# The first batch's counting products dealt between the raw groups' products of a graph layer

## The chip, the cores and the metric

The kernel runs on one core of a Trainium2 chip. The metric is the device time of one execution in microseconds; of several runs the median is taken. TensorE is called PE in the profile, its weight loads PEld, VectorE DVE, ScalarE ACT, GpSimd POOL, and the queue of SyncE that issues plain transfers SP.

## The reference

There are 12500 nodes with 128 features and 200000 edges, sorted by their target. Every row of x is normalized and clipped at zero; every edge takes the row of its source through the matrix of its type (four types, 128 x 128) and adds the result, with the type's bias, to its target; x itself is added.

```python
h = jnp.maximum(_layernorm(x, axis=-1), 0.0)
xs = h[src]
for i in range(4):
    mask = (edge_type == i)[:, None]
    msgs = msgs + jnp.where(mask, xs @ W[i] + b[i], 0.0)
out = x + jax.ops.segment_sum(msgs, dst, num_segments=N)
```

The targets are drawn with a square, so the first few hundred nodes receive many edges each and the last ones few.

## The kernel before, in words

Edges are cut into chunks of 128. The first 512 chunks, whose targets have many edges, are handled as **dense** work; the other 1051 chunks go by **groups** of 16 (at the end smaller ones).

**The table.** At the start every row of x is normalized and split into three bf16 parts, and written to a table in device memory, htab (`first_part` to `third_part`, L481 to L508). While it is made, `make_slots` (L797) sorts the dense edges into slots of at most 128 edges of one target; loT and hkT hold, for each slot, where the sources of its edges lie.

**Raw groups.** The first three groups (RAW = 3) don't wait for the table. Their rows come straight from x (`gather_raw`, L525, tile hx), and `add_up_raw` (L610) does the rest for each group in steps that are separated by `yield`: statistics on DVE (L440 to L449), a one-hot matrix ohf on DVE (L620); then the scales (L455, L456) and 16 normalizing instructions on ACT (L461); then four times four f32 products of 16 edge chunks on PE (L635), each four copied from PSUM to SBUF by ACT (L636); then the counts of edges per type (L641, copied by L643), and last the bias and the four type matrices (L646, L648), which add into one PSUM bank, raw_py. Two PSUM banks (pool s_ps) take the results of L635 and L641 in turn. A copy on ACT (L1283) brings raw_py to SBUF, and DVE adds it to a ring of target columns later (L666).

**Dense work.** It goes in 18 batches, the first of 17 units and the others of 27. `count` (L938) makes for each slot two one-hots on DVE (o2 at L957, o1 at L961 or L965) and one **counting product** on PE (L983, 128 x 396 columns); a unit is two to four slots in one PSUM bank, copied to the batch's counts tile by ACT (L989). The one-hots go through four sets of buffers of four slots (SETS, SLOTS): a set is made ahead, and one is made again when PE has used it. The first batch has 34 slots. `multiply` (L1021) then streams the whole table from device memory in tiles hs (L1029, four buffers) and multiplies it with the counts (L1033). `dense_work` (L1094) deals the counting of a batch and the multiplying of the batch before it into one stream; each step of it returns the share of the dense work that is done. A slot of the first batch, which has no multiplying beside it, counts 3.5 times in that share.

**The loop.** From group 3 on, each group gathers the rows of its chunks from htab on POOL (`gather`, L538, L544; 12 buffers of two chunks), makes 16 one-hots on DVE (L561), multiplies on PE (`sum_up`, L569, L578), and is weighed one group later (`weigh`, L586: L596, L600, L603, L605); DVE adds the results to the ring (L666). After each two chunks the loop draws steps of the dense work until the share done has come up to `pace` (L1079), which spreads the dense work evenly over the loop. The loop's instructions on PE, DVE and ACT run in the order in which they are written (`manual_schedule`, L1302); what stands ahead of it, the raw groups among it, is ordered by the scheduler.

**Memory.** SBUF is given out by pools that stand on two stacks, a left and a right one. What is needed only at the start lies on the left (early: prep, nodes, aheads, raws) and is freed at L1269; the pools of the loop (outp, later, dense with two counts tiles, sdp, op1, op2, hsp) then take its place on the left. So a tile of theirs must wait for the last reader of the early tile that lay there; the raw rows (pool raws, L247) were the topmost. Two of the waits are of interest: the load of the loop's first block of edge data (`prep_steps`, L306, into pool later; read on DVE by L319 to L329) and DVE's third ohf, of which there are two buffers (L619).

Of the kernel before, what the change touches and what calls it, by code (L numbers as in the profile page):

```python
# [35 lines left out]
F32 = mybir.dt.float32  # L36
# [3 lines left out]
I32 = mybir.dt.int32  # L40
# [8 lines left out]
P = 128  # L49
EPS = 1e-5  # L50
UN = 3
G = 16
# [4 lines left out]
UB = 27  # L57
# [4 lines left out]
STREAM = 4  # L62
# [3 lines left out]
HG = 2  # L66
RAW = 3
LEAD = RAW
SOON = (RAW * 16) + HG

TURN = 4


@with_exitstack
def kernel(
# [170 lines left out]
    aheads = early.enter_context(tc.tile_pool(name="aheads", bufs=4))  # L246
    rawp = early.enter_context(tc.tile_pool(name="raws", bufs=RAW * G // HG))  # L247

# [137 lines left out]
    nc.vector.tensor_single_scalar(iota_1, iota_b, 1.0, op=ALU.add)  # L386
    iota_f = prep.tile([P, KR], F32, name="iota_f", bufs=1)
    nc.vector.tensor_copy(iota_f, iota_i[:, :KR])
# [28 lines left out]

    pick_f = prep.tile([P, NT, N3], F32, name="pick_f", bufs=1)
    nc.vector.tensor_copy(pick_f, pick)
# [190 lines left out]
    def add_up_raw(t0, g, rows, marked):  # L610
# [7 lines left out]
        root()  # L618
        oh = rawp.tile([P, G, KR], F32, name="ohf", bufs=2)[:, :, :K]  # L619
        nc.vector.tensor_tensor(  # L620
# [473 lines left out]
    def dense_work():  # L1094
# [8 lines left out]
        for vs in batches + [None]:  # L1103
            steps, led = {}, {}
            now = None
            if vs:
                now = vs, dense.tile([P, NW + 1, UB * NT], I32, name="counts")
                steps[count(*now)] = sum(len(slots_of(u)) for u in vs) * (a_slot if before else alone_slot)
            if before:
                passed = multiply(*before)  # L1110
                steps[passed] = 3 * len(before[0]) * a_node
                led = {passed: BEHIND}
            done = {st: 0.0 for st in steps}
            while done:
                st = min(done, key=lambda st: done[st] + led.get(st, 0.0))
                part = next(st, None)
                if part is None:
                    del done[st]
                    gone += steps[st]
                else:  # L1120
                    done[st] = part
                    yield (gone + sum(done[st] * steps[st] for st in done)) / total
            before = now
# [9 lines left out]
    hkT = slots.tile([P, NS], F32, name="hkT")  # L1133
    byT = slots.tile([P, (ND - PAIRS) // 2], F32, name="byT")
    building = ExitStack()
    dix = building.enter_context(tc.tile_pool(name="dix", bufs=1, side="right"))
# [129 lines left out]
    for g in groups:  # L1266
        for _ in g:
            pass
    early.close()  # L1269
# [4 lines left out]
    counting = mid.enter_context(ExitStack())  # L1274
    dense = counting.enter_context(tc.tile_pool(name="dense", bufs=2))
    sdp = counting.enter_context(tc.tile_pool(name="sdp", bufs=1))
# [3 lines left out]
    nc.vector.memset(o2s[:, :, :, NB:], 1.0)  # L1280
    hsp = counting.enter_context(tc.tile_pool(name="hsp", bufs=STREAM))
    raw_sums = outp.tile([P, OT, D], F32, name="xo").rearrange("p j d -> p (j d)")[:, : RAW * G * win_raw]
    nc.scalar.copy(raw_sums, raw_py[:, : RAW * G * win_raw])  # L1283
    raw_adds = [
# [17 lines left out]
    ordered.enter_context(tc.manual_schedule(engines={mybir.EngineType.PE, DVE, mybir.EngineType.Activation}))  # L1302
    assert min(goes) >= RAW
    for gi, (t0, g) in list(enumerate(zip(starts, sizes)))[RAW:]:
        q = (t0 + 8 * G) // P
# [15 lines left out]
        for j, part in enumerate(sum_up(t0, g, *now, gi >= FULL)):  # L1321
            late, tails[:] = list(tails), []
            while work and spent < pace(gi, part):
                spent = next(work, None)
                if spent is None:
                    work = None
# [194 lines left out]
```

## Time and profile before

| | us |
|---|---|
| median of the runs shown (1666.21, 1667.36, 1667.64) | 1667.36 |
| the profiled execution | 1663.02 |
| its span in the profile | 1661.2 |
| PE busy in it | 1417.4 (85%) |
| DVE busy | 1014.6 (61%) |
| ACT busy | 446.9 (27%) |
| POOL busy | 1030.6 (62%) |
| mean granted clock of PE | 0.958 |

The span is the time from the first to the last instruction that the profile shows. A line of a timeline has start, duration, engine, line of the kernel, operation, tiles, shape and count, and in brackets how long the engine sat idle before it and what ended that. The f32 products stand as two records each. Records of PE are pipelined: the distance from one start to the next is what one costs, not its duration. A line of busy time by stretch has the stretch, its length, the busy time and count of PE, PEld, DVE, ACT and POOL, the granted clock as a share of the full one, the share of the DMA engines and GB/s.

### The profile page before, as it was taken

To read this page: it belongs to the slowest core of one execution; us is meant where nothing else is said; L and a number is where in the kernel's file an instruction comes from. 1 tells how busy PE (TensorE), PEld (TensorE's weight loads), DVE (VectorE), ACT (ScalarE), POOL (GpSimd) and SP (SyncE) were. 2 spreads that over 40 slices of the span, in tenths; PEclk is the share of its full clock that TensorE was granted. 3 is DMA by queue.
4 is the path that set the end of the run, shared out by engine and by line. 5 is a ranking of instruction groups with operands and counts; after the bars stand their busy time and mean duration, and the time that the engine had idled before them with its cause. 6 is when DMAs were issued, how large, how long until landed. Compare 5 with 4: busy or idle time off the path is not lost.

```text
span 1661.2 us, 32454 instructions
## 1 busy us (share of the span) xinstructions
PE 1417.4 (85%) x10984; PEld 921.7 (55%) x10984; DVE 1014.6 (61%) x5305; ACT 446.9 (27%) x1095; POOL 1030.6 (62%) x1078
## 2 busy tenths in 40 slices
PE   3868798988888889898979899998898889898975
PEld 1336565655555556565555556565565555555644
DVE  6982877647474746574756565666466556563433
ACT  5694222221212122222222222222222222222111
POOL 6435666666666666666666666666666666666562
PEclk9986899999999999999999999999999999999997
DMA  6552476665665656656656565665565556556652
GB/s 204 168 197 75 153 229 194 205 212 185 196 205 182 200 176 211 204 184 199 202 168 199 185 194 187 198 194 188 190 205 185 193 185 193 185 181 192 206 165 63
DMA packets 136761, 308.90 MB, mean 186 GB/s; under 512 B 25899, under 2 KB 78813, under 8 KB 136590
## 3 DMA queue, kind: packets, MB, share of 16 engines
q1 hardware_dynamic: 86909, 204.98, 37.8%
q0 software_dynamic: 49680, 101.81, 20.4%
q8 instruction: 86, 1.41, 0.3%
q14 instruction: 86, 0.70, 0.1%
HBM read 290.65 MB, written 16.04 MB: 185 GB/s over the span
## 4 chain that ended last, share of the span: by engine, by line
PE 74%; DVE 11%; issue 9%; another core or an unknown queue 2%; ACT 1%; DMA 1%; POOL 0%; SPq 0%; DVEq 0%; ACTq 0%; POOLq 0%
PE pa L1033 43%; PE pt L983 11%; PE ps L578 6%; PE py L605 6%; DVE o L957 2%; DVE o L965 2%; PE pt L1047 1%; DVE ring L666 1%; DVE oh L561 1%; PE ps L635 1%; PE py L596 1%; PE pt L691 1%; DVE stt L440 1%; POOL hm L544 0%
## 5 line engine op out<-in xcount | busy, mean ns | idle before, releaser
L544 POOL DMA_INDIRECT hm<-htab,srcT x1003 | 975.0, 972 | 565.5 <-issue 230.9
L1033 PE MATMUL pa<-counts,hs 128*128 128x324 fp8e4 (+1 forms) x5292 | 963.3, 305 | 79.2 <-issue 69.7
L1033 PEld LDWEIGHTS <-hs 128*128 128x128 bf16 x5292 | 492.3, 97 | 353.9 <-issue 132.7
L957 DVE TENSOR_SCALAR o<-iota_n,hkT 128x392 bf16<-128x392 f16 x1167 | 385.0, 330 | 75.2 <-PE pt L983 30.2
L983 PE MATMUL pt<-o,o 128*128 128x396 bf16 x1167 | 369.5, 337 | 40.3 <-DVE o L965 21.4
L989 ACT CAST counts<-pt 128x396 int32<-128x396 f32 x476 | 228.5, 493 | 479.4 <-PE pt L983 149.0
L561 DVE TENSOR_SCALAR oh<-iota_b,keyT 128x56 bf16<-128x56 bf16 (+8 forms) x1003 | 172.8, 260 | 294.6 <-PE ps L578 101.3
L581 ACT COPY sb<-ps 128x224 f32<-128x224 f32 (+8 forms) x251 | 99.4, 397 | 544.5 <-PE pt L983 172.5
L578 PE MATMUL ps<-oh,hm 128*128 128x56 bf16 (+8 forms) x3009 | 192.1, 197 | 38.9 <-issue 32.7
L666 DVE TENSOR_TENSOR ring<-ring,py 128x14 f32 (+7 forms) x976 | 171.9, 176 | 84.4 <-remote 17.3
L578 PEld LDWEIGHTS <-hm 128*128 128x128 bf16 x3009 | 165.2, 99 | 100.4 <-issue 55.1
L965 DVE TENSOR_SCALAR o<-iota,loT 128x128 bf16<-128x128 bf16 x644 | 177.2, 275 | 0.0
L983 PEld LDWEIGHTS <-o 128*128 128x128 bf16 x1167 | 111.3, 98 | 98.9 <-issue 30.2
L965 DVE TENSOR_SCALAR o<-iota,loT,byT 128x128 bf16<-128x128 bf16 x417 | 142.0, 340 | 0.0
L605 PE MATMUL py<-sb,wsb 128*128 128x224 f32 (+7 forms) x488 | 128.3, 402 | 5.5 <-issue 5.3
L605 PEld LDWEIGHTS py<-sb,wsb 128*128 128x128 f32 x488 | 86.4, 190 | 32.9 <-issue 11.7
L528 POOL DMA_INDIRECT hx<-in_x_dram,srcT x48 | 50.1, 1044 | 36.8 <-DVE stt L440 13.1
L997 DVE COPY bi<-counts 128x27 int32<-128x27 int32 (+1 forms) x18 | 4.1, 225 | 107.2 <-ACT counts L989 60.5
L600 ACT CAST cnt<-py 128x224 bf16<-128x224 f32 (+7 forms) x61 | 24.1, 395 | 103.7 <-PE ps L578 35.6
L461 ACT ACTIVATE h<-hm,nmrt,rstdt 128x128 f32<-128x128 f32 x98 | 42.8, 492 | 0.9 <-issue 0.5
L490 PE MATMUL ps<-h,ident 128*128 128x384 f32 (+1 forms) x34 | 17.2, 591 | 15.7 <-issue 11.4
L596 PE MATMUL py<-oh,three 128*32 128x224 bf16 (+7 forms) x244 | 21.2, 311 | 7.6 <-issue 3.9
(234 smaller groups left out, 650.2 us busy)
## 6 DMA issues: line engine op xcount, KB each, us to landing
hs<-htab SPq DMA_DIRECT2D x288, 576.0 KB
hm<-htab,srcT POOLq DMA_INDIRECT x1003
htab<-h SPq DMA_DIRECT2D x32, 288.0 KB
xo<-in_x_dram SPq DMA_DIRECT2D x23, 256.0 KB
out_dram<-xo SPq DMA_DIRECT2D x23, 256.0 KB
hm<-in_x_dram SPq DMA_DIRECT2D x18, 192.0 KB
hs<-htab SPq DMA_DIRECT2D x18, 192.0 KB
hm<-in_x_dram SPq DMA_DIRECT2D x14, 168.0 KB
```

What stands on the lines that cost most here:

```text
L528: one = nc.gpsimd.indirect_dma_start(out=hm[:, i * D : (i + 1) * D], out_offset=None, in_=x, in_offset=bass.IndirectOffsetOnAxis(ap=srcf[: ...
L544: one = nc.gpsimd.indirect_dma_start(out=hm[:, (i - h0) * D3 : (i - h0 + 1) * D3], out_offset=None, in_=htab, in_offset=bass.IndirectOffse ...
L561: nc.vector.tensor_scalar(oh[:, i, :], iota_b[:, :K], keyf[:, at : at + 1], None, ALU.is_equal)
L578: nc.tensor.matmul(ps[:, i - i0, :], rows(i, c), oh[:, i, :], start=(c == 0), stop=(c == 2))
L581: nc.scalar.copy(sb[:, i0:i1].rearrange("p g t n -> p g (t n)"), ps[:, : i1 - i0, :])
L605: nc.tensor.matmul(py[:, :g, :], wsb[:, t, :], sb[:, :g, t, :], start=False, stop=(t == NT - 1))
L666: nc.vector.tensor_tensor(to, to, of(i), ALU.add)
L957: one = nc.vector.tensor_scalar(o2[:, k, :NB], iota_n, hkT[:, s : s + 1], None, ALU.is_equal)
L965: one = nc.vector.tensor_scalar(o1[:, k], iota_1, loT[:, s : s + 1], by, ALU.is_equal, ALU.mult)
L983: one = nc.tensor.matmul(pb, o1, o2, start=first, stop=last)
L989: nc.scalar.copy(counts[:, :, i * NT : (i + 1) * NT], pb.rearrange("p (b t) -> p b t", t=NT))
L1033: nc.tensor.matmul(pa[:, : 3 * nu * NT].rearrange("p (m v) -> p m v", m=3), hs[:, j - j0, c * D : (c + 1) * D], of, start=(j == 0 and c == 0),
```

## The change

The pool of the raw rows moves to the right stack, below the pool of the slots' making, and gets a third ohf buffer; iota_f and pick_f, which the raw groups read, become constants. Ahead of the loop each raw group is taken through two steps only (statistics and one-hot; scales and normalizing). Its other six steps are taken after the order written by hand has begun, and after each of them two steps of the dense work are drawn (AMONG = 2), 32 of the first batch's 34 in all: two counting products after each four raw products, after L641 and after L648. The raw rows are then freed, and only then the second counts tile (dense2) and the hs buffers are given out. `pace` is stretched over the share that is left.

```diff
+AMONG = 2
...
-    rawp = early.enter_context(tc.tile_pool(name="raws", bufs=RAW * G // HG))
...
-    iota_f = prep.tile([P, KR], F32, name="iota_f", bufs=1)
+    iota_f = const.tile([P, KR], F32, name="iota_f")
...
-    pick_f = prep.tile([P, NT, N3], F32, name="pick_f", bufs=1)
+    pick_f = const.tile([P, NT, N3], F32, name="pick_f")
...
-        oh = rawp.tile([P, G, KR], F32, name="ohf", bufs=2)[:, :, :K]
+        oh = rawp.tile([P, G, KR], F32, name="ohf", bufs=RAW)[:, :, :K]
...
-                now = vs, dense.tile([P, NW + 1, UB * NT], I32, name="counts")
+                now = vs, dense[batches.index(vs) % 2].tile([P, NW + 1, UB * NT], I32, name="counts")
...
+    raw_stack = ExitStack()
+    rawp = raw_stack.enter_context(tc.tile_pool(name="raws", bufs=RAW * G // HG, side="right"))
...
     for g in groups:
-        for _ in g:
-            pass
+        next(g)
+        next(g)
...
-    dense = counting.enter_context(tc.tile_pool(name="dense", bufs=2))
...
-    hsp = counting.enter_context(tc.tile_pool(name="hsp", bufs=STREAM))
+    dense = [counting.enter_context(tc.tile_pool(name="dense", bufs=1))]
...
-    nc.scalar.copy(raw_sums, raw_py[:, : RAW * G * win_raw])
...
+    first_slots = sum(len(slots_of(u)) for u in batches[0]) - 2
+    for g in groups:
+        for _ in g:
+            for _ in range(max(0, min(AMONG, first_slots))):
+                spent = next(work)
+            first_slots -= AMONG
+    nc.scalar.copy(raw_sums, raw_py[:, : RAW * G * win_raw])
+    raw_stack.close()
+    dense.append(counting.enter_context(tc.tile_pool(name="dense2", bufs=1)))
+    hsp = counting.enter_context(tc.tile_pool(name="hsp", bufs=STREAM))
+    ahead_of = spent
...
-            while work and spent < pace(gi, part):
+            while work and spent < ahead_of + (1.0 - ahead_of) * pace(gi, part):
```

## Prediction

> **What bounds the kernel now.** I read the page first, then busy time by stretch, then the timelines of PE, DVE and ACT from 110 to 200 us, where the diff acts.
>
> ```profile
> span 1661.2 us, 32454 instructions
> PE 1417.4 (85%) x10984; PEld 921.7 (55%) x10984; DVE 1014.6 (61%) x5305; ACT 446.9 (27%) x1095; POOL 1030.6 (62%) x1078
> ```
>
> PE is the bound over the whole run (85%). The change adds and removes no product, so it can win only PE idle time and PE time at the half clock. Where these lie near the edit:
>
> ```profile
> 120.00:150.00 30.00, 29.14 (x122) 24.90 (x122) 0.83 (x1) 16.61 (x48) 18.36 (x20) 0.50 0.25 72
> 150.00:155.40 5.40, 4.02 (x20) 2.76 (x19) 0.23 (x1) 0.77 (x2) 2.42 (x3) 0.50 0.39 103
> 155.40:180.60 25.20, 13.13 (x110) 6.44 (x108) 19.28 (x97) 9.32 (x24) 16.53 (x17) 0.84 0.29 80
> 180.60:200.00 19.40, 17.81 (x171) 14.44 (x171) 18.73 (x103) 4.58 (x13) 13.01 (x14) 0.92 0.60 191
> ```
>
> The columns are PE, PEld, DVE, ACT and POOL busy, then the granted clock. From 120 to 150 the raw groups run: PE is busy 29.14 of 30 us, but at clock 0.50, and DVE does nothing (0.83). From 155.4 to 180.6 it is the reverse: DVE is busy 19.28 of 25.2, and PE sits idle 12.1 us. Why DVE was idle and then late:
>
> ```profile
> 127.60 0.83 DVE L620 TENSOR_TENSOR ohf<-iota_f,keyT 128x640 f32<-128x640 f32 x1 [7.87 <-PE ps L641]
> 154.16 0.23 DVE L319 CAST sf<-si 128x128 f32<-128x128 int32 x1 [25.74 <-DMA si<-in_src_dram]
> 156.50 0.15 DVE L320 CAST head<-di 128x1 f32<-128x1 int32 x1 [2.11 <-DMA di<-in_dst_dram]
> 158.14 0.32 DVE L957 TENSOR_SCALAR o<-iota_n,hkT 128x392 bf16<-128x392 f16 x1
> 158.59 0.32 DVE L957 TENSOR_SCALAR o<-iota_n,hkT 128x392 bf16<-128x392 f16 x1
> ```
>
> L620 waits for a third ohf buffer; then L319 waits 25.74 us for a load into memory that lay under the raw rows. Behind it in DVE's queue stand the one-hots of the counting products, one slot per 0.45 us (158.14 to 158.59). So the first batch's 34 slots come at DVE's pace, after the raw stage.
>
> **The change, part by part.** P is four raw products, S is two counting products, pc is L641, py is L646 with L648. The rows that price them:
>
> ```profile
> 114.91 3.63 PE L635 MATMUL ps<-ohf,hx 128*128 128x40 f32 x16 [2.44 <-ACT hx L461]
> 120.86 3.64 PE L635 MATMUL ps<-ohf,hx 128*128 128x40 f32 x16 [2.31 <-ACT hx L461]
> 124.42 2.31 PE L641 MATMUL ps<-ohf,pick_f 128*12 128x160 f32 x8
> 126.66 1.93 PE L635 MATMUL ps<-ohf,hx 128*128 128x40 f32 x8
> 128.53 0.31 PE L646 MATMUL pa<-cnt,b 12*128 12x160 bf16 x1
> 128.76 2.50 PE L648 MATMUL pa<-sb,wsb 128*128 128x160 f32 x8
> 131.06 5.31 PE L635 MATMUL ps<-ohf,hx 128*128 128x40 f32 x24
> 148.04 2.31 PE L641 MATMUL ps<-ohf,pick_f 128*12 128x160 f32 x8
> 152.71 0.29 PE L646 MATMUL pa<-cnt,b 12*128 12x160 bf16 x1 [1.38 <-ACT cnt L643]
> 157.07 0.67 PE L983 MATMUL pt<-o,o 128*128 128x396 bf16 x3
> 157.57 0.31 PE L578 MATMUL ps<-oh,hm 128*128 128x40 bf16 x6
> ```
>
> At clock 0.50, from start to start: P 1.78 us (half of 120.86 to 124.42; two records a product), pc 2.24, py 2.53 (128.53 to 131.06). At full clock a counting product takes 0.167 us (157.07 to 157.57, three of them), so S is 0.33 us, and 0.66 at half. In full, P is 0.89, pc 1.12, py 1.27.
>
> *ACT's new order (a loss).* Each group is now run through its normalizing (two steps) before any product, so on ACT all 48 L461 stand ahead of the first copy of a result (L636). Before, only 16 did:
>
> ```profile
> 114.37 6.27 ACT L461 ACTIVATE hx<-hx,nmrr,rstdr 128x128 f32<-128x128 f32 x16 [0.18 <-DVE nmrr L456]
> 120.54 0.45 ACT L636 COPY sb<-ps 128x160 f32<-128x160 f32 x2
> 127.59 0.28 ACT L643 CAST cnt<-ps 12x160 bf16<-12x160 f32 x1 [1.79 <-PE ps L641]
> 152.38 0.28 ACT L643 CAST cnt<-ps 12x160 bf16<-12x160 f32 x1 [3.94 <-PE pt L983]
> ```
>
> One L461 takes 0.385 us ((6.27 - 0.49)/15), 48 of them from 114.37 last to 133.0, and with one copy the third P starts at 133.3 instead of 120.86. The result banks are two, so PE does two P and two S by 120 and then waits 13 us. Nothing hides this.
>
> *Raw stage on PE.* Group 0 has left two P with S, pc, S, py, S. Between pc and py the copy L643 comes; it started 0.93 us after pc's end in one group (126.66 to 127.59) and 2.1 in another (148.04 + 2.24 = 150.28 to 152.38), S hides 0.66, so a gap of 0 to 1.8; I take 0.6, and 1.0 where no S stands. At half clock: 2 x 2.44 + 2.24 + 0.66 + 0.6 + 2.53 + 0.66 = 11.6, to 144.9. The rest hangs on the clock, next. Full: group 1 takes 4 x 1.22 + 1.12 + 0.33 + 0.6 + 1.27 + 0.33 = 8.5, group 2 (its last two steps carry no S) 4.9 + 1.1 + 1.0 + 1.3 = 8.3, and the stage ends at 161.7. Half: 16.5 and 15.5, end 176.9. Before, it ended at 155.2 (2.5 after 152.71).
>
> *The clock.*
>
> ```profile
> 139.33:142.74 3.41, 3.41 (x15) 3.19 (x15) 0.00 (x0) 3.41 (x10) 2.54 (x3) 0.50 0.18 49
> 152.98:156.40 3.42, 3.42 (x18) 2.78 (x18) 0.23 (x1) 1.31 (x3) 1.55 (x2) 0.50 0.68 186
> 159.81:163.22 3.41, 1.76 (x20) 0.99 (x20) 3.41 (x19) 0.69 (x2) 2.50 (x4) 1.00 0.26 70
> 163.22:166.64 3.42, 1.23 (x12) 0.54 (x11) 3.42 (x19) 0.59 (x2) 2.81 (x3) 1.00 0.31 85
> 1641.20:1644.61 3.41, 3.41 (x18) 2.67 (x16) 1.15 (x2) 0.51 (x1) 0.00 (x0) 0.50 0.27 77
> ```
>
> The granted clock changes only at steps of 3.413 us. For every such window I counted the columns put through (f32 twice) against what the window's clock could carry. The 20 half-clock windows that ended at half had a share of 0 to 0.74 (139.33 is the 0.74); the 20 after which it rose had 0.78 to 1.15 (152.98 has 0.90, the last, 1641.20, has 1.04). At full clock, 159.81 (0.45) kept it and 163.22 (0.22) lost it; the losing ones lie at 0.46 and below, 19 of 21 at 0.36 and below, and after the first 20 us of the run none that kept it lies under 0.38. PE's busy time doesn't tell these apart, the columns do. P alone has a share of 0.30 (8 records x 80 columns in 1.78 us, at 396/0.33 = 1.2 columns a ns), so the raw stage never rose. With S it is (640 + 792)/2928 = 0.49: too little to rise, enough to keep. But S, pc, S in a row is 3.56 us at 0.97, and py, S nearly as long: wherever the window falls, one of them mostly fills it. So I take a rise in group 0's pc or py, about 145, kept from there: three chances in four.
>
> The Trainium skill (TensorE: Matmul & The Clock Gate, "What's actually happening") says instead that about 3.4 us of sustained activity of the PE releases the throttle. By that rule the 29.14 busy us above would not have stayed at 0.50; the trace disagrees, and the rule's own result is a rival below.
>
> *After the raw stage.* What before has done at 180.6 beyond the raw groups is some 46 counting products and 66 L578 (42 and 60 from 155.4 on, and a few ahead). The changed kernel still has 14 and 66 of them.
>
> ```profile
> L578 PE MATMUL ps<-oh,hm 128*128 128x40 bf16 x60 | 3.4, 191 | 0.0
> L561 DVE TENSOR_SCALAR oh<-iota_b,keyT 128x56 bf16<-128x56 bf16 (+8 forms) x1003 | 172.8, 260 | 294.6 <-PE ps L578 101.3
> 169.65 1.40 DVE L666 TENSOR_TENSOR ring<-ring,xo 128x10 f32 x7
> ```
>
> PE: 14 x 0.167 + 66 x 0.057 = 6.1. DVE has its one-hots 12 or so slots ahead (four sets of buffers), and still owes L319 to L329 (1.9), 16 L561 (2.8 at 0.17) and 7 adds (1.4), 6.1 as well. I take 6.5. That is 161.7 + 6.5 = 168.2 against 180.6: **12.4 us earlier**. It counts as won the PE stall that ends there:
>
> ```profile
> 175.90 0.85 PE L983 MATMUL pt<-o,o 128*128 128x396 bf16 x4 [1.28 <-DVE o L965]
> 180.59 0.67 PE L1033 MATMUL pa<-counts,hs 128*128 128x204 fp8e4 x3 [3.84 <-issue]
> 178.34 0.29 ACT L600 CAST cnt<-py 128x160 bf16<-128x160 f32 x1 [3.79 <-remote]
> 180.05 0.89 ACT L989 CAST counts<-pt 128x396 int32<-128x396 f32 x2
> ```
>
> L1033 needs the last L989 of the first batch, which stood in ACT's queue behind L600 (178.34); the first of the two ends at 180.54, and L1033 starts at 180.59. In the new order that L989 is ahead of any L600.
>
> *The queues.* The four hs loads now wait until the raw rows are free:
>
> ```profile
> 112.63 1.75 SPq L1029 DMA_DIRECT2D hs<-htab x4
> L544 POOL DMA_INDIRECT hm<-htab,srcT x24: 940/946/1080, 114.7 to 149.6; - x24
> ```
>
> Before, SP issued them at 112.63. Now it is at the last pc, some 2.5 us before the stage's end, and the first L1033 comes some 3 us after it. A cost of 0 to 4 us; I take 2. SP has nothing urgent behind them. POOL's 24 gathers into 12 buffers were done by 150.5 and are as early now; the later ones wait for L578, as before. The side load (si, ty, di) moves ahead of two table writes on SP and is long landed. Bringing iota_f and pick_f to the constants, and the split of the counts into two pools, issue nothing new.
>
> Sum: -12.4 + 2 = **-10**. The other 1480 us keep their order and work (the dense share per group falls as the first batch is gone, by as much as was moved). The profiled execution took 1663.0 us (span 1661.2), so 1653; the median shown is 1667.4, some 4 above it, and I apply the 10 to that: **1657.4**.
>
> **Rivals.**
> 1. *The clock never rises in the raw stage (slower).* Price: end at 176.9, + 6.5 + 1.7 for a window at half + 2 = 187.1 against 180.6, **+6.5: 1674**. For: P with S has 0.49, and gaps before py near 1.8 empty the windows; against: S, pc, S leaves only some phases under 0.75. It decides where the stage ends after 172.
> 2. *The rise comes only in group 1.* End near 169.5, so -2 to -3: **1665**, the idle 13 us ahead having eaten the gain.
> 3. *The 3.84 us stall comes again*, since its root, a late L600, may be of PE's and not of this order: -6, **1661**.
> 4. *PE rises on busy time alone*, in the first window after 133.3, by 138.2: group 0's pc on at full, end at 158.6, 3.1 earlier: -13, **1654**. The row of 120 to 150 speaks against it. It is what the rule of the Trainium skill (TensorE: Matmul & The Clock Gate, "What's actually happening") would give.
>
> **How the numbers follow.** Forecast 0.42, rival 1 0.20, rival 2 0.15, rival 3 0.18, rival 4 0.05. A measurement can tell about 0.2% (3.3 us). Faster: 0.42 + 0.18 + 0.05 = 0.65; same: rival 2, 0.15; slower: rival 1, 0.20. The forecast's own range is 1653 to 1661 (L643's gap 0 to 1.8 in three groups, the loads 0 to 4). To leave out no more than 2 in 10 the range goes to 1652 below, and above into rival 1, to 1671.
>
> **What would show it.** ACT: 48 L461 without a copy among them, ending near 133. PE: a gap of about 13 us from 120, L983 between L635 from then on, last L648 near 162 (or 177). The clock: 1.00 by 145 to 148; if it is 0.50 up to 170, rival 1 holds. DVE: no wait of 25 us at L319. First L1033 some 3 us after the last L648, with no stall of 3.8 us; if it waits for hs, the loads were late. If the stage ends near 162 and the gain is still missing, DVE is the bound after it, and my 6.5 us were wrong.

## The result, and the profile after

The changed kernel is slower: 1692.7 us median (1687.4 to 1694.2) against 1667.5 (1666.2 to 1668.6), 1.0146 times, 95% interval 1.0128 to 1.0163. Its profiled execution took 1687.4 us, 24.4 more than that of the kernel before. The prediction said 10 us less, and its range ended at 1671.

The page of the changed kernel shows no more work, only more time in which PE waits:

```profile
span 1685.7 us, 32466 instructions
PE 1420.3 (84%) x10984; PEld 922.9 (55%) x10984; DVE 1019.6 (60%) x5305; ACT 448.2 (27%) x1095; POOL 1033.0 (61%) x1078
```

ACT's timeline in the raw stage (start, duration, engine, line, tiles, count, and in brackets the idle time ahead with its cause) has the 48 L461 in one row, as forecast, and then something that was not forecast:

```profile
115.47 18.57 ACT L461 ACTIVATE hx<-hx,nmrr,rstdr 128x128 f32<-128x128 f32 x48 [0.33 <-DVE nmrr L456]
...
149.02 0.29 ACT L636 COPY sb<-ps 128x160 f32<-128x160 f32 x1 [11.64 <-remote]
150.43 0.49 ACT L989 CAST counts<-pt 128x396 int32<-128x396 f32 x1 [1.11 <-remote]
150.81 0.28 ACT L643 CAST cnt<-ps 12x160 bf16<-12x160 f32 x1
```

PE's timeline beside it:

```profile
134.27 1.93 PE L635 MATMUL ps<-ohf,hx 128*128 128x40 f32 x8 [13.38 <-ACT sb L636]
136.00 0.86 PE L983 MATMUL pt<-o,o 128*128 128x396 bf16 x2
136.65 1.77 PE L635 MATMUL ps<-ohf,hx 128*128 128x40 f32 x8
...
151.14 0.29 PE L646 MATMUL pa<-cnt,b 12*128 12x160 bf16 x1 [9.05 <-ACT cnt L643]
...
174.68 1.35 PE L648 MATMUL pa<-sb,wsb 128*128 128x160 f32 x8
175.87 0.31 PE L578 MATMUL ps<-oh,hm 128*128 128x40 bf16 x6
...
178.34 0.43 PE L1033 MATMUL pa<-counts,hs 128*128 128x204 fp8e4 x3
```

There are two gaps. The first, 13.38 us, is ACT's row. The second, 9.05 us, is odd: by its records PE was through with the fourth four raw products (from 136.65) by 138.4, and ACT copied them only at 149.02 ("remote": the profile finds no instruction that ended this wait). The clock came late as well. Busy time by stretch (columns as in the prediction):

```profile
134.00:151.00 17.00, 7.82 (x30) 5.12 (x31) 0.57 (x3) 2.82 (x11) 9.84 (x11) 0.50 0.25 67
151.00:166.00 15.00, 14.86 (x61) 11.60 (x60) 5.74 (x26) 4.37 (x12) 0.00 (x0) 0.50 0.01 2
166.00:176.00 10.00, 9.57 (x76) 7.74 (x75) 4.22 (x20) 4.38 (x11) 0.00 (x0) 0.97 0.09 12
```

So the raw stage ended at 176.0, not at 161.7. Yet the dense work, on which the prediction was built, is not late: the first L1033 comes at 178.34, and in the kernel before it came at 180.59. What is late is the loop. Its first copy of a group's counts stood at 178.34 in the kernel before; here it is

```profile
203.04 0.29 ACT L600 CAST cnt<-py 128x160 bf16<-128x160 f32 x1 [1.25 <-PE ps L578]
```

24.7 us later, and the last L600, 64 groups on, is 24.5 us later (1650.9 and 1675.4). All that was lost was lost by the first group. The engine that shows where is the one that the prediction passed by, POOL, which gathers the loop's rows. POOL's timeline, first before, then after:

```profile
149.58 0.95 POOL L544 DMA_INDIRECT hm<-htab,srcT  x1 [0.30 <-issue]
152.63 0.95 POOL L544 DMA_INDIRECT hm<-htab,srcT  x1 [2.10 <-PE pt L983]
```

```profile
145.93 0.95 POOL L544 DMA_INDIRECT hm<-htab,srcT  x1 [0.30 <-issue]
176.45 0.95 POOL L544 DMA_INDIRECT hm<-htab,srcT  x1 [29.56 <-PE ps L578]
```

Twelve buffers of two chunks hold 24 gathers; the 25th needs a buffer that a first L578 has freed. In the kernel before the scheduler had put six L578 right behind the last L641, ahead of the last L646:

```profile
150.28 0.38 PE L578 MATMUL ps<-oh,hm 128*128 128x40 bf16 x6
```

In the changed kernel the first L578 comes after the whole stage, at 175.87. So POOL stood still for 29.56 us instead of 2.10, and the 25th gather is 23.8 us later (152.63, 176.45). From it to the end of the span it is 1508.6 us before and 1509.2 after.

### The profile page after: what moved, and what is told of

It is laid out like the page before. It is cut to its first block, busy times and chain, and to the rows that moved or that the text cites. A ratio compares the mean times of both kernels' runs of the same rounds, so it can differ in the third digit from the quotient of the medians.

```text
span 1685.7 us, 32466 instructions
## 1 busy us (share of the span) xinstructions
PE 1420.3 (84%) x10984; PEld 922.9 (55%) x10984; DVE 1019.6 (60%) x5305; ACT 448.2 (27%) x1095; POOL 1033.0 (61%) x1078
## 4 chain that ended last, share of the span: by engine, by line
PE 78%; issue 11%; DVE 5%; ACT 3%; another core or an unknown queue 2%; DMA 0%; DVEq 0%; SPq 0%; ACTq 0%
PE pa L1033 44%; PE pt L983 12%; PE ps L578 7%; PE py L605 7%; PE pt L1047 1%; PE py L596 1%; ACT hx L461 1%; DVE ring L666 1%; PE pt L691 1%; PE ps L635 1%; PE ps L490 1%; DVE o L957 1%; PE pt L857 1%; ACT h L461 1%
## 5 line engine op out<-in xcount | busy, mean ns | idle before, releaser
L1033 PE MATMUL pa<-counts,hs 128*128 128x324 fp8e4 (+1 forms) x5292 | 968.3, 305 | 83.1 <-issue 80.4
L1033 PEld LDWEIGHTS <-hs 128*128 128x128 bf16 x5292 | 492.9, 97 | 362.6 <-issue 140.5
L983 PE MATMUL pt<-o,o 128*128 128x396 bf16 x1167 | 370.6, 339 | 37.4 <-issue 28.0
L578 PE MATMUL ps<-oh,hm 128*128 128x56 bf16 (+8 forms) x3009 | 196.2, 198 | 47.9 <-issue 43.5
L578 PEld LDWEIGHTS <-hm 128*128 128x128 bf16 x3009 | 166.4, 99 | 106.4 <-issue 60.9
L983 PEld LDWEIGHTS <-o 128*128 128x128 bf16 x1167 | 113.0, 99 | 92.9 <-issue 43.4
L600 ACT CAST cnt<-py 128x224 bf16<-128x224 f32 (+7 forms) x61 | 24.1, 396 | 97.6 <-PE ps L578 29.9
L461 ACT ACTIVATE h<-hm,nmrt,rstdt 128x128 f32<-128x128 f32 x98 | 42.8, 492 | 1.6 <-DVE vart L446 1.2
L635 PE MATMUL ps<-ohf,hx 128*128 128x40 f32 x96 | 18.4, 358 | 16.0 <-ACT sb L636 13.4
```

The costliest lines, as they stand in the source:

```text
L461: return nc.scalar.activation(h, xt(k), AF.Relu, bias=nmr[:, k : k + 1], scale=rstd[:, k : k + 1]).ins
L578: nc.tensor.matmul(ps[:, i - i0, :], rows(i, c), oh[:, i, :], start=(c == 0), stop=(c == 2))
L983: one = nc.tensor.matmul(pb, o1, o2, start=first, stop=last)
L1033: nc.tensor.matmul(pa[:, : 3 * nu * NT].rearrange("p (m v) -> p m v", m=3), hs[:, j - j0, c * D : (c + 1) * D], of, start=(j == 0 and c == 0),
```

## The experiments

The runs fell on several chips of two kinds, which can't be left out of their reading: the kernel before took 1667 us on those of the result and of e1 to e4, 1692 on that of e5 to e8, and 1418 to 1419 on those of e9 to e18. Each ratio is to the kernel before on the same chip. The table takes the 25th gather from POOL's timeline and the span from the page of each. The kernel before itself was profiled on one chip alone, so times in us are compared with care across chips. The ratio of e6 is from three of its four executions; the fourth took 3423 us.

| kernel | times before (95%) | 25th gather | span | from it to the end |
|---|---|---|---|---|
| before | 1 | 152.63 | 1661.2 | 1508.6 |
| changed | 1.0146 (1.0128 to 1.0163) | 176.45 | 1685.7 | 1509.2 |
| e1 old pace | 1.0126 (1.0101 to 1.0150) | 175.80 | 1685.9 | 1510.1 |
| e2 in turn | 1.0112 (1.0076 to 1.0149) | 169.86 | 1678.9 | 1509.0 |
| e3 late gathers | 1.0264 (1.0236 to 1.0292) | 192.01 | 1707.6 | 1515.6 |
| e4 memory only | 1.0007 (0.9995 to 1.0019) | 155.98 | 1666.7 | 1510.7 |
| e5 less dense | 0.9961 (0.9947 to 0.9975) | 155.67 | 1683.7 | 1528.0 |
| e6 fewer gathers | 0.9151 (0.9115 to 0.9188) | 156.18 | 1548.9 | 1392.7 |
| e7 first group ahead | 1.0162 (1.0145 to 1.0179) | 161.88 | 1717.2 | 1555.3 |
| e8 in turn and ahead | 1.0111 (1.0087 to 1.0136) | 155.36 | 1701.6 | 1546.2 |
| e9 in turn, ties | 0.9995 (0.9977 to 1.0012) | 138.29 | 1414.2 | 1275.9 |
| e16 the same | 1.0008 (0.9984 to 1.0032) | 147.11 | 1422.2 | 1275.1 |
| e10 before, no ties | 1.0004 (0.9991 to 1.0018) | 140.91 | 1416.9 | 1276.0 |
| e15 the same | 0.9996 (0.9981 to 1.0010) | 139.66 | 1416.9 | 1277.2 |
| e18 the same | 1.0001 (0.9991 to 1.0011) | 140.80 | 1417.8 | 1277.0 |
| e11 changed, one more tie | 1.0036 (1.0023 to 1.0049) | 147.57 | 1424.5 | 1276.9 |
| e13 changed | 1.0045 (1.0032 to 1.0059) | 147.40 | 1422.0 | 1274.6 |
| e14 changed, pairs | 1.0135 (1.0111 to 1.0159) | 163.61 | 1436.9 | 1273.3 |
| e17 the same | 1.0135 (1.0117 to 1.0154) | 165.85 | 1434.9 | 1269.1 |
| e12 before, 14 buffers | 0.9978 (0.9969 to 0.9988) | 136.51 | 1413.5 | 1277.0 |

**What the end hangs on: e1, e4.** e1 undoes the stretching of the pace:

```diff
-            while work and spent < ahead_of + (1.0 - ahead_of) * pace(gi, part):
+            while work and spent < pace(gi, part):
```

> The changed kernel, but the pace of the loop isn't stretched: the loop draws dense work only when the old pace has passed the share that the raw stage has already done, so the first loop group gets almost none. Theory A (the loop is a chain of groups of about 24.3 us each, whatever 1 or 2% of dense work each carries; the changed kernel is late because its first loop group starts after the raw stage, takes a full 27 us with its share of dense work, and 24.5 us late it stays): the first loop group becomes 10 to 18 us shorter and the time falls with it, to 1675 to 1683 us. Theory B (only the sum of PE's work and how well it is packed count, and the loop packs worse since its loads and gathers take longer): dense work that isn't done in the first group has to be done later, so no gain, 1689 to 1697.

Neither theory came out clean. The first loop group, freed of dense work, ended 10.1 us earlier (its L600 at 192.96 instead of 203.04), as theory A said. Then PE stood still for 12 us. It is the second gap again. POOL gathered from 175.80 to 198.2 without a break, and the L983 that PE had done by 188.44 by its records was announced only at 199.89 (the semaphore update in the trace); DVE, which waits for PE's counting products, shows "remote":

```profile
187.93 0.51 PE L983 MATMUL pt<-o,o 128*128 128x396 bf16 x1 [0.23 <-issue]
200.46 0.67 PE L1033 MATMUL pa<-counts,hs 128*128 128x204 fp8e4 x3 [12.01 <-issue]
```

```profile
199.92 0.32 DVE L957 TENSOR_SCALAR o<-iota_n,hkT 128x392 bf16<-128x392 f16 x1 [18.27 <-remote]
```

The next group's L600 was at 225.88, against 227.0 in the changed kernel, and the gain was gone; so e1 doesn't decide by itself whether the chain of groups or something else sets the end. The 25th gather had moved by 0.65 us only, and the end by 0.2. That gave the theory that the later runs test (S): the stream of gathers sets the time.

e4 keeps the new places in memory and undoes the dealing, and has the old pace:

```diff
     for g in groups:
-        next(g)
-        next(g)
+        for _ in g:
+            pass
...
-    for g in groups:
-        for _ in g:
-            for _ in range(max(0, min(AMONG, first_slots))):
-                spent = next(work)
-            first_slots -= AMONG
```

> The new places in memory alone: raw rows on the right stack, third ohf buffer, second counts tile and hs buffers given out late, but the raw groups run through as before, with no counting products among them and the old pace. Theory M (the new places of hs and counts make loads and gathers slower in the loop: 4608-byte packets took 237 ns on average there instead of 222): 1680 to 1692. Theories A and B: DVE's waits for ohf and for the side load are gone, raw stage and first loop group come as before or a few us earlier, 1658 to 1669.

1.0007: the places in memory cost nothing (theory M missed), and the end of DVE's waits brings nothing. The 25th gather comes at 155.98, 20 us ahead of the changed kernel's.

**What sets the loop: e5, e6.** e5 leaves out products of the dense part, e6 gathers, both in the kernel before.

```diff
                 for c in range(3):
+                    if c == 1 and j % 3 == 1:
+                        continue
```

> The kernel before, with one in nine of the products L1033 left out (588 of 5292, so the dense sums are wrong; 588 x 0.143 us = 84 us of PE). It asks what sets the length of the loop. Theory S (the stream of gathers sets it: in the first six profiles the time from the 25th gather to the end was 1508.6, 1509.2, 1510.1, 1509.0, 1515.6 and 1510.7 us, whatever dense work was moved about): 1640 to 1668 us. Theory P (PE's work sets it): 1575 to 1600.

```diff
+            if h0 == 4 * HG:
+                got.append(got[-1])
+                continue
             hm = hpool.tile([P, HG * D3], BF16, name="hm")
```

> The kernel before, with one tile of gathered rows in eight not gathered but the tile before it used twice (about 125 of 1003 gathers left out, so those edges bring wrong rows; PE's products stay all). Theory S: 978 gathers at 1.515 us after the 24th become 856, about 185 us less, until PE's own work stops it: PE is busy 1298 of the 1480 us from 180 on, so 1500 to 1600 us. Theory P: within 10 us of before, 1656 to 1670.

84 us less of PE's work brought 0.39%, 6 us, as S said. An eighth fewer gathers brought 8.5%, some 140 us, less than the 185 that S allowed and far from the nothing of theory P. In 600 us of the loop, by stretch, e5, e7 (on the same chip, with all its products) and e6:

```profile
400.00:1000.00 600.00, 508.55 (x4034) 325.02 (x4033) 372.01 (x1973) 136.63 (x335) 380.16 (x390) 0.97 0.63 191
```

```profile
400.00:1000.00 600.00, 519.70 (x4239) 340.07 (x4239) 366.44 (x1944) 134.69 (x332) 378.69 (x391) 0.99 0.62 190
```

```profile
400.00:1000.00 600.00, 563.78 (x4676) 375.22 (x4675) 403.37 (x2138) 152.38 (x368) 365.06 (x376) 0.99 0.66 201
```

The fifth group of numbers is POOL: 390 and 391 gathers in the same time, though PE had 205 products fewer to do in e5. With fewer gathers PE does more in the same time (4676 products). PE is the busiest engine of the loop, and its work is not what sets the loop's length. POOL's work alone isn't either on these chips: in the kernel before it waits 237 us in all for buffers from its 25th gather on, beyond the 0.30 us that stand between any two gathers. So the stream is a ring in which POOL waits for buffers that PE frees, and PE's results are seen late beside gathers (below); which part of the ring would have to become faster these two runs don't tell.

**The raw stage: e2, e3.** e2 writes the normalizing in turn:

```diff
-        done = [normalize(k, row(k)) for k in range(g)]
...
+        norms.extend([lambda k=k: normalize(k, row(k)) for k in range(g)])
...
             first_slots -= AMONG
+            for f in norms[:SG]:
+                f()
+            del norms[:SG]
```

> The changed kernel, but the normalizing of a raw group's rows (L461) is written in turn, eight rows ahead, then four after each step of the raw stage, so that no copy of a result stands behind 48 of them on ACT. PE's gap of 13 us before the third four raw products should be gone on either theory. ACT has 48 x 0.385 + 12 x 0.28 + 17 x 0.49 = 30 us of work from 114.4 on, so the stage can't end before about 147; before it ended at 155.2, in the changed kernel at 176. If nothing else holds PE: end at 148 to 152, the first loop group's L600 near 177, and 1664 to 1670 us by theory A and by theory B. If the second gap of the changed kernel (9 us, PE's products done but seen late by ACT and DVE while POOL's gathers run) comes again: stage end about 9 later, 1673 to 1679.

ACT's gap of 13 us went, and gaps of the second kind grew: 4.89 us ahead of an L647 (L646 of the listing) and 10.29 ahead of raw products, while POOL gathered without a break until 147:

```profile
133.35 0.28 PE L647 MATMUL pa<-cnt,b 12*128 12x160 bf16 x1 [4.89 <-ACT cnt L644]
...
151.46 1.93 PE L636 MATMUL ps<-ohf,hx 128*128 128x40 f32 x8 [10.29 <-ACT sb L637]
```

The stage ended at 169.4, 6.6 us earlier, and the span fell by 6.8. Stage and time (1683.1 us) both lie beyond what either case expected. e3 took the gathers out of the raw stage:

```diff
-    rows = gather(RAW * G, G)
...
-    nc.scalar.copy(raw_sums, raw_py[:, : RAW * G * win_raw])
+    summed = nc.scalar.copy(raw_sums, raw_py[:, : RAW * G * win_raw])
+    gates[:] = [summed.ins]
+    rows = gather(RAW * G, G, RAW * G)
```

> The changed kernel, but the gathers of the first loop group are held until the last raw result has been copied, so POOL issues nothing from 114 us to the end of the raw stage. Theory G (the 9 us in which PE's ends are seen late come from the gathers that run beside it): that gap is gone, P4's copy follows its products within 0.3 us, and the stage ends near 167 instead of 176. Rival N (the gap has another cause, the order or the half clock): the gap of 8 to 10 us stands at the same place. In time: the 16 gathers of the first group now take 20 us after the stage, about as long as that group took anyway (27 us), so by G 1682 to 1690, by N 1691 to 1705.

The second gap is gone, and the clock rises in the last products of group 0:

```profile
143.71 0.31 PE L646 MATMUL pa<-cnt,b 12*128 12x160 bf16 x1
143.95 1.93 PE L648 MATMUL pa<-sb,wsb 128*128 128x160 f32 x8
145.72 0.50 PE L983 MATMUL pt<-o,o 128*128 128x396 bf16 x2
146.06 0.98 PE L635 MATMUL ps<-ohf,hx 128*128 128x40 f32 x8
...
160.65 1.35 PE L648 MATMUL pa<-sb,wsb 128*128 128x160 f32 x8
```

Two L983 in 0.34 us instead of 0.65: full clock from 145.7, and the stage ends at 162.0. So on this chip it is the gathers, whether their issue on POOL or their transfers, that hold PE up. The time is far worse (1.0264, beyond what was expected), because 23 of the 24 gathers now stand behind the stage, one each 1.25 us, and PE starves a second time beside them:

```profile
180.93 0.33 PE L1033 MATMUL pa<-counts,hs 128*128 128x204 fp8e4 x1 [1.83 <-issue]
181.64 0.49 PE L983 MATMUL pt<-o,o 128*128 128x396 bf16 x1 [0.37 <-issue]
183.74 0.33 PE L1033 MATMUL pa<-counts,hs 128*128 128x204 fp8e4 x1 [1.61 <-issue]
184.44 0.33 PE L1033 MATMUL pa<-counts,hs 128*128 128x204 fp8e4 x1 [0.37 <-issue]
```

One product each 0.7 to 2.1 us, for which the profile shows no wait. e3 also parts the end of the raw stage from the stream of gathers: the stage ended 14.0 us earlier than in the changed kernel, the 25th gather came 15.6 us later, and the span is 21.9 us longer. So the end follows the gathers and not the stage.

How long a row of gathers runs seems to be what makes the gap. In the raw stage the longest time from the recorded end of a product to the next semaphore update is 10.6 us in the changed kernel, 9.9 in e1, 12.4 in e2, 11.6 in e7 and 10.5 in e8; in all five the 24 gathers ran in one row of 30 us, and the late product ended 20 to 24 us after the row's start. In the kernel before, e4, e5 and e6, whose ties leave rows of at most nine gathers, it is 1.9 to 2.2 us, and in e3, with one gather in the stage, 0.015. But the five are also those with counting products among the raw ones, so no run of these chips changes the rows alone.

**Letting POOL go on: e7, e8.** Twelve chunks of the first loop group are multiplied between the raw steps:

```diff
+    loop_first, parts_ahead, turn = sum_up(RAW * G, G, rows, oh, False), [], 0
...
             first_slots -= AMONG
+            turn += 1
+            if turn > 7 and turn % 2 == 0 and len(parts_ahead) < G // HG - 2:
+                parts_ahead += [next(loop_first), next(loop_first)]
```

> The changed kernel, but 12 of the 16 chunks of the first loop group are multiplied (L578) between the steps of the second and third raw group, 4 after every second step, so that buffers come free and POOL goes on gathering before the raw stage ends. Theory S: the 25th gather comes near 158 instead of 176.5, and the time is that plus 1509: 1665 to 1676 in the profile, and as much less than 1692 in the median (1670 to 1680), although the same work and order of the dense part stand after it. Theory P: the raw stage only gets longer by 36 products and their waits: 1690 to 1698.

> Both edits: normalizing in turn and 12 chunks of the first loop group between the raw steps. Theory S: the 25th gather near 153 (as in the kernel before: 152.6), so 1659 to 1670 us. Theory P: 16 us less than the changed kernel as with normalizing in turn alone, 1680 to 1686.

Both expectations by S missed, and those by P, taken as shares of 1667.5 (1.014 to 1.018 and 1.008 to 1.011), were met: 1.0162 and 1.0111. e7's 25th gather came at 161.88, 14.6 us earlier than in the changed kernel, but after 12 more POOL was out of buffers again:

```profile
176.63 0.95 POOL L544 DMA_INDIRECT hm<-htab,srcT  x1 [0.30 <-issue]
201.93 0.96 POOL L544 DMA_INDIRECT hm<-htab,srcT  x1 [24.34 <-PE pt L983]
```

The second pause comes from the edit: the loop draws the dense work of the chunks that were multiplied ahead in one go, in front of the next L578 (in e7 from 187.75 to 201.35, in e8 from 176.13 to 189.73). The 37th gather tells the loss: 173.75 in e5, which starts as the kernel before and ran on the same chip, 201.93 in e7 and 190.31 in e8, so 28.2 and 16.6 us later, where the medians are 27.5 and 17.4 us above that of the kernel before. So S holds in a wider form, that a pause of POOL ahead of the steady loop is lost wherever it lies. This form was made after the result, and these two runs don't rule P out.

**Without the stall: e9 to e18.** The chips of these runs show no stall of PE beside gathers. The semaphore updates in the trace say how large the difference is: between 178 and 1620 us the next update came on average about 1.0 us after the recorded end of a product in the kernel before (some 1400 of them; 0.9 to 1.1 by how one counts), and 0.04 us in e13.

> The changed kernel once more, beside the others of this call. On a chip with PE's stall under gathers: second gap of 6 to 11 us before L646, raw stage 18 to 22 us later than in the kernel before, 1.012 to 1.017 times. On a chip without it (as in e9 to e12): no second gap, the clock rises in group 0's last products as forecast, raw stage ends near 147, 25th gather 7 to 10 us later than in the kernel before, and 1.003 to 1.008 times, since the loop is only the stream of gathers.

Here the raw stage goes much as the prediction had it, and the kernel is still slower, 1.0045 (1.0032 to 1.0059), 6.5 us:

```profile
120.88 1.93 PE L635 MATMUL ps<-ohf,hx 128*128 128x40 f32 x8 [13.31 <-ACT sb L636]
...
128.64 0.31 PE L646 MATMUL pa<-cnt,b 12*128 12x160 bf16 x1
128.88 1.99 PE L648 MATMUL pa<-sb,wsb 128*128 128x160 f32 x8
...
146.82 0.31 PE L578 MATMUL ps<-oh,hm 128*128 128x40 bf16 x6
```

From the third four raw products to the end of the stage it is 25.9 us; the forecast had 28.4 (133.3 to 161.7). POOL's 25th gather, in e13 and then in e15, the old order on the same chip:

```profile
147.40 0.94 POOL L544 DMA_INDIRECT hm<-htab,srcT  x1 [13.63 <-PE ps L578]
```

```profile
139.66 0.94 POOL L544 DMA_INDIRECT hm<-htab,srcT  x1 [6.14 <-PE ps L578]
```

7.7 us later, and the medians are 7.3 us apart (1425.69, 1418.41). e11 was meant to break up the row of gathers, by one more tie (each tile's first gather waits for the gather before it). The tile's second gather had no such tie, and no break came about: from 108 us on its gathers stand 0.30 us apart. It is in effect a second run of the changed kernel, 1.0036, less than it expected for breaks.

```diff
                 if i == h0 and gates and t0 + i >= SOON:
                     held_by(one, gates.pop(0), "the first rows come while the slots are made, not ahead of them")
+                if i == h0 and landed and t0 + i < (RAW + 1) * G + 4 * HG:
+                    held_by(one, landed[-1], "two gathers at a time, with a break")
+                landed.append(one.ins)
```

> The changed kernel, nothing else moved, but in the first 24 gathers each pair waits until the pair before has landed, a break of about 1.3 us after every two. Theory B: the 13 us gap for ACT stays, the 9 us gap after it goes, the clock rises at 145 to 150 as forecast, the raw stage ends at 162 to 166 and so does the row of gathers; 25th gather at 163 to 167, so 1.006 to 1.010 times before. Rival C (any gather beside it holds PE up, so much for each): the same delay in smaller pieces, stage end 172 or later, 1.012 to 1.018.

e14 and e17 tie both gathers of a tile to the tile before:

```diff
+                if h0 == i:
+                    last_pair = list(landed[-1:])
+                if last_pair and t0 + i < (RAW + 1) * G + 4 * HG:
+                    held_by(one, last_pair[0], "two gathers at a time, with a break")
+                landed.append(one.ins)
```

> The changed kernel with both gathers of a tile held until the tile before has landed, for the first 24 gathers: 2.5 us of gathers, 1 to 1.3 us of break. Theory B (a long row of gathers makes the stall): no second gap on either kind of chip; raw stage ends 26 to 30 us after ACT's gap; with the row itself ending near 45 us after its start, 1.005 to 1.010 times before on a chip with the stall, 1.003 to 1.010 on one without. Rival C (any gather delays PE): on a chip with the stall the gap stays 5 us or more, 1.012 to 1.018.

> As e14, the changed kernel with a break after every two of the first 24 gathers. On a chip with the stall, theory B: no second gap before L646 (under 1 us), the clock rises in group 0's last products, the raw stage ends 26 to 30 us after ACT's gap, as on the chips without the stall, and the row of gathers ends near 165 to 172 and sets the 25th; 1.006 to 1.014 times before. Rival C: the gap of several us is there in spite of the breaks. On a chip without the stall: as e14, 1.011 to 1.016.

They ask about the stall, and could not answer that here. They answer S instead (e14's 25th gather):

```profile
163.61 1.05 POOL L545 DMA_INDIRECT hm<-htab,srcT  x1 [0.30 <-issue]
```

Raw stage and dense order are those of e13 (the last L648 starts at 146.77 in e17, at 145.62 in e13), only the row of 24 gathers ends later, and the time is 1.0135 times before. That is more than e14 expected (1.003 to 1.010), because each break took 2.4 us and the row 60. On one chip, e14's 25th gather comes 16.2 us after e13's and its median is 12.9 us higher: most of such a pause is paid, not quite all.

e10, e15 and e18 take the ties out of the kernel before, so that its first 24 gathers run in one row.

```diff
-    gates.extend(ties + marks[len(marks) - (20 - 1 - len(ties)) :])
```

> The kernel before without the ties between gathers and normalizing, so that its first 24 gathers run in one row from 114.7 to about 145. Theory B: its raw stage, which is otherwise unchanged, now shows PE's ends seen late by several us, and ends 3 to 12 us after 155.4; 1.002 to 1.008 times before. Rival: the row does no harm of its own (the harm needs the counting products and their four banks): raw stage ends at 153 to 156, 0.998 to 1.001.

> As e10, the kernel before with its first 24 gathers in one row. On a chip with the stall, theory B: PE's ends seen late by 5 us or more in its raw stage, 25th gather 3 to 12 us later, 1.002 to 1.008. Rival: no harm, 0.998 to 1.001. On a chip without the stall: 1.000 within 0.0015, as e10.

> As e15, the kernel before with its first 24 gathers in one row. On a chip with the stall, theory B: ends of PE's products seen late by 5 us or more in its raw stage, which then ends later than 155.4 after the same start, 25th gather 3 to 12 us later than in the kernel before, 1.002 to 1.008. Rival: no harm, 0.998 to 1.001. On a chip without the stall 1.000 within 0.0015.

No difference (1.0004, 0.9996, 1.0001), as expected of a chip without the stall (e10 had not foreseen the chip, and its rival held); what a row alone does on the other kind is left open.

e9 and e16 are e2 with these ties put back, each pair of gathers behind every fifth normalizing:

```diff
-            for f in norms[:SG]:
-                f()
-            del norms[:SG]
+            normalize_next(SG)
+            while ties and tiles_of:
+                gates[:] = [ties.pop(0)]
+                gather(RAW * G, G, got_rows, [tiles_of.pop(0)])
```

> Normalizing in turn as in e2, and the gathers of the first loop group held again by every fifth normalizing instruction, as in the kernel before, so that they come in short bursts spread over the raw stage. Theory B (what holds PE in the raw stage is a long unbroken row of gathers on POOL: with 24 in a row PE's products and ends stood still for 9 to 10 us): raw stage ends at 150 to 158 instead of 169.6 (e2), the 25th gather there, and that plus 1509: 0.996 to 1.003 times before. If e2's stalls have another cause, they come again: stage end near 168, 1.009 to 1.013.

> As e9, normalizing in turn and ties on the gathers. On a chip with the stall, theory B: raw stage 10 to 18 us shorter than e13's, 25th gather within 5 us of the kernel before's, 0.997 to 1.004. If the stalls don't depend on the row: 1.008 to 1.013. On a chip without the stall: 0.998 to 1.001 as e9.

0.9995 and 1.0008: on these chips the dealing with normalizing in turn costs nothing and brings nothing. The ties didn't break the row: in both profiles the 24 gathers stand 0.3 to 0.53 us apart. The two profiles, from two chips, differ by 8.0 us in the span and by 8.8 in the 25th gather (138.29, 147.11). Only e9's gather is about where the old order on its chip has it (140.91 in e10); e16's is 7.5 us later than in e15, the old order on its chip, and its profiled execution took 1423.89 us against 1418.69. The last raw group in e9, then in e16:

```profile
131.00:138.00 7.00, 6.58 (x56) 5.37 (x55) 3.44 (x17) 3.48 (x10) 2.45 (x3) 1.00 0.33 77
```

```profile
131.00:138.00 7.00, 7.00 (x33) 6.34 (x33) 2.58 (x12) 2.05 (x5) 3.88 (x4) 0.50 0.28 70
```

In e16 the clock had fallen to half before it and the alternation of P and S did not raise it again. e16's ten executions, all on one chip, fall apart accordingly: four took 1411.8 to 1417.9 us at a mean granted clock of 0.972 to 0.980, six took 1423.2 to 1425.8 at 0.966 to 0.971.

e12 changes two sizes of the kernel before, 14 buffers of rows instead of 12, and 3 of hs instead of 4 to make room.

```diff
-STREAM = 4
+STREAM = 3
...
-    hpool = mid.enter_context(tc.tile_pool(name="rows", bufs=12))
+    hpool = mid.enter_context(tc.tile_pool(name="rows", bufs=14))
```

> The kernel before with 14 buffers of gathered rows instead of 12, and 3 hs buffers instead of 4 to make room. After the 25th gather POOL is idle 305 us beyond the 0.3 us between two gathers, mostly for buffers. Theory S1 (the stream waits for buffers, and more of them let it run ahead): 0.97 to 0.993 times before. Theory S2 (buffers only pass on PE's pace, and PE is held by the gathers themselves, so a faster stream would hold PE longer): 0.997 to 1.004; three hs buffers could make it slower, to 1.02.

0.9978 (0.9969 to 0.9988): the only version with all its work that is faster than the kernel before, by 3 us. S accounts for it: with 28 gathers' room the 25th didn't wait and came at 136.51, 4.4 us earlier than in e10 on the same chip, and the rest took as long (1277.0, 1276.0). After that POOL waits only 8 us for buffers there; on the other kind of chip, where it waits 237, 14 buffers were not tried. (The 305 us of the expectation is too much: part of the 0.30 us gaps is counted in it.)

## Why the prediction was wrong

**The step that failed** is "After the raw stage": "What before has done at 180.6 beyond the raw groups is some 46 counting products and 66 L578", priced at PE's and DVE's time for what is still missing, 6.5 us. As an account of the dense work it was good: the changed kernel reached its first L1033 2.3 us after the stage. As an account of the loop it left out the one thing that is hardly ever caught up, how far the stream of gathers has come. The queue part had the fact in hand ("the later ones wait for L578, as before") and didn't ask when that L578 comes: it had stood at 150.28, inside the raw stage, and the new order put it behind the stage. The runs show in its place the 25th gather, 23.8 us later with the span 24.5 us longer. Some 9.5 us of that belong to this step: had the stage ended at 161.7 as forecast, the 25th gather would have come near 162 and the span ended near 1671 (an estimate: 162 and the 1509 us that follow in both kernels), 10 us later than before. On a chip where the stage did go as forecast (e13) the kernel is 6.5 us slower. So the sign was lost here. The other 14.3 us are the raw stage's own, below.

**"The other 1480 us keep their order and work"** was true of the order, and the conclusion was not: a little less dense work in each group was to shorten each, and a loop that is paced by gathers hardly notices (e5). The opening sentence, that PE is the bound at 85% and that one can win only PE's idle time and half clock, read the share of busy time as the limit. Gathers at 1.515 us each (978 from 152.63 to 1634.02) were in that profile.

**ACT's new order** was right: last of 48 L461 at about 133, PE idle 13 us; measured 13.38, all of it 1 us later.

**The raw stage on PE**: durations right, end 14.3 us late (176.0 against 161.7). About 1.0 is the later start; 8.4 the second gap (9.05, where 0.6 had been allowed); 4.0 group 1's four P and S at half clock (2.22 us each, where 1.22 was forecast); the rest its last products. The second gap is the gathers': shown by e3, which takes them out of the stage and has no gap. With the old order the ties had broken the 24 gathers into rows of nine, six and nine (114.73 to 150.5); with the L461 in one row the ties came free early, and the gathers ran in one row from 116.45 to 146.9. That the length of the row is what counts agrees with nine profiles (above) and was not shown by an edit of the row alone, since e10, e14, e15, e17 and e18 fell on chips without the stall.

**The clock** was right in kind. Without the gap, S, L641, S and the products after them raised it within group 0 (e3 at 145.7, e13 between 128.9 and 132.3). With the gap the windows of 3.41 us around it were empty or partly filled, and the rise came a group later. The rival by which busy time alone raises the clock, in the Trainium skill (TensorE: Matmul & The Clock Gate, "What's actually happening"), does not fit the row of 151 to 166 above: PE busy 14.86 of 15 us, clock 0.50.

**The rivals.** Rival 1 had the stage's end to within a microsecond (176.9 against 176.0), by luck: it had half clock in all three groups and no second gap, where the run had the gap, half clock up to about 166 and full clock after it. It gave 1674, for it used the same 6.5 us. Rival 3's stall did not come, and neither did a wait for the hs loads (cost 0, I had taken 2). No rival had POOL in it, so no range could reach the measured 1692.7.

## What to carry to other kernels

Before moving work to fill an engine's idle time, find which stream sets the steady state: leave out a part of each engine's work and see which cut shortens the run; the busiest engine need not be it. Then follow that stream through the edit, above all the first instruction that frees a buffer for it, since most or all of a pause of the stream ahead of the steady state is paid. And an order in which one engine's queue takes a whole stage at once (48 L461) also moves everything that was tied to it, here the gathers' spacing.

## What the runs showed of the hardware

- A gather of 128 rows holds POOL 0.98 us, and the next starts 0.30 us later at the earliest. In e15 it is 1.288 us a gather over the whole loop (978 from 139.66 to 1399.83), and POOL's waits beyond the 0.30 us come to 12 us, so on this chip the stream runs at POOL's own pace. PE is busy there for 591.55 of 600 us as well (400 to 1000 us), so a faster stream alone need not win much. The Trainium skill (DMA: Bandwidth & Descriptors, "Anatomy of one DMA — SWDGE (gpsimd) path") calls the generation of descriptors a small and variable part of such a transfer's fixed cost. What of the 0.98 us is that generation no run here shows; for a stream of gathers the measured 1.28 us each are the price.
- The kernel before takes 1667 and 1692 us on some chips and 1418, 15 to 16% less, on others. Where it is slow, PE's results are seen about 1.0 us late on average beside gathers, and 10 to 12 us once in the raw stage of each run with 24 gathers in a row (138.4 to 149.0 in the changed kernel); where it is fast, 0.04. What makes the chips differ stays open.
- One program on one chip can have two times some 8 us apart, and they go with the mean granted clock (e16: about 1416 us at 0.976 and 1424 at 0.968). That it depends on where the clock's windows fall is an inference from the two profiles of e9 and e16.
